# A two-layer adaLN and mixture-of-experts kernel: two-sided decayed sums as a scan of a scan, the shared expert's rows stored as a second summand, routing pieces a step later, VectorE's order written out

## The chip, the cores and the metric

The kernel runs on one core of a Trainium2 chip. The metric is the device time of one execution in microseconds (us). One launch computes everything. The engines are named as in the profile: PE is TensorE's matrix unit (PEld its weight loads), DVE is VectorE, ACT is ScalarE, POOL is GpSimd and SP is SyncE, which here only issues transfers.

## The reference, cut to what matters

There are two layers over x of shape 4 x 512 x 512 (2048 tokens of 512 channels). Each layer first mixes along time, per channel and batch, with a sum that decays in both directions, then runs a mixture of experts and adds the result to x.

```python
def _bi_wkv(r, k, v, w, u, time_emb):          # k and v are the same side input
    tf = sigmoid(sum(time_emb, -1))[:, None, None]
    decay = exp(-exp(w))[None, :] * (0.5 + 0.5 * tf[:, :, 0])
    ek = exp(minimum(k, 30.0)); ekv = ek * v
    # a = a * decay + ekv_t; b = b * decay + ek_t, forward (nf, df) and in reverse (nb, db)
    euk = exp(minimum(u + k, 30.0))
    num = nf + nb - ekv + euk * v
    den = df + db - ek + euk
    return sigmoid(r) * (num / maximum(den, 1e-8)) * (0.8 + 0.2 * tf)

x = x + L0_ffn(L0_cond(x, ...))   # rmsnorm, router to 2 of 8 experts (256 wide), plus a shared expert
x = x + L1_ffn(L1_cond(x, ...))   # router to 6 of 32 experts (352 wide, 512 slots each), plus a shared one
```

## The kernel before, in words

All arithmetic is in float32. The side input is kept turned, channels on partitions, in `kA` (128 x 4 x 2048); the rows of x lie in `acc` (16 tiles of 128 rows). A unit is one batch b and one group c of 128 channels, so a layer has 16 units of 128 x 512.

**Layer 0, the loop over units (L641).** Step n holds pieces of several units. `turn(n + 3)` turns the side input on PE and ACT copies it to `kA`. `front(n + 1)` makes two clamped copies on DVE and `front_exps(n + 1)` takes their exponentials on ACT. `mid(n)` makes two products and four scans on DVE (`scans`, L259): forward and reverse, for the denominator and the numerator, into four tiles. `sums(n - 1)` adds three terms each for `den` and `num` on PE by matmuls with a diagonal matrix (L436 to L438), and ACT then takes a reciprocal in three passes (`r`, L440 to L442). `back(n - 1)` finishes the unit with four operations on DVE (L449 to L452). `num` has one PSUM bank, so the next `num` waits for L451. Between these stand, at fixed steps: `sigmoids` of the next batch; `row_turn` and `row_out` (rows back and stored to `z0d`); `logits0`; the routing of a finished batch in five parts (`route_v`, `route_max`, `route_top`, `route_pos` with `route_pay`, `route_slots`), the last of which writes eight indirect transfers to `table0` from POOL; and the shared expert (`share_up`, `share_silu`, `share_hid`, `share_turn`, `share_down`, `share_add`) for tiles 0 to 5, in pairs that begin at steps 7, 10 and 13. `share_add` adds the shared result to the row of x on DVE and stores the sum to `xa`. A second summand, `xb`, is filled with zeros at the start, by 16 stores on POOL's queue.

**The tail of that stage (L694 to L735).** The last batch is routed; tiles 6 to 12 of the shared expert run; the table is read back; some exponentials of layer 1 (`exps1_upto`) are taken, for which ACT changes its function table and changes it back.

**The routed stage of layer 0 (`routed`, L740).** For each expert, tiles of 128 slots: POOL gathers rows from `z0d` into rows 8 to 15 of `acc` (L768), PE turns them (L781), ACT copies with a scale (L785), PE makes gate and up (L833, L837), POOL multiplies the hidden row (`hrow`, L844), PE turns it (L795) and makes the output (L809), ACT copies it (L811) and POOL adds it by an indirect transfer alternately to `xa` and `xb` (L814). Beside that, DVE runs `wkv1` (L907), the two-sided sums of layer 1, for all 16 units.

**After it.** Three late tiles of the shared expert, then the sum of `xa` and `xb` and layer 1's gating (L962 to L985), the shared expert of layer 1, and its routed stage, which fills the second half of the time.

**What sets the order.** In the first stage the program order of ACT, PE and DVE is kept by hand (`manual_schedule`, L192); POOL and SP are ordered by a planner. In the routed stage of layer 0 POOL, PE and ACT are kept by hand and DVE is ordered by the planner (L936). Each engine runs its queue in order. The transfers of SP share one queue: `load_k` has one buffer `kr`, so the load of the next batch is issued only when all four groups of the present one have been turned.

Of the kernel before, what the change touches and what calls it, by code (L numbers as in the profile page):

```python
# [18 lines left out]
P = 128  # L19
# [6 lines left out]
DEN_MIN = 1e-8  # L26
EXP_LN = "natural_log_exp_and_others"
# [3 lines left out]
def adaln_ffn_kernel(  # L31
# [90 lines left out]
    def load_k(b):  # L122
        kr = wk.tile([P, TB, D], F32, tag="kr", name=f"kr{b}", bufs=1)
        nc.sync.dma_start(kr, kf[b * S : (b + 1) * S, :].rearrange("(i p) c -> p i c", p=P))
        return kr
# [54 lines left out]
    kr = wk.tile([P, TB, D], F32, tag="kr", name="kr0", bufs=1)  # L180
    for i in range(TB):
        nc.scalar.dma_start(kr[:, i, :], kf[i * P : (i + 1) * P, :])
    load_x(0)
    gaten = acc[:E1, NT - 3, :]
# [9 lines left out]
            engines={mybir.EngineType.Activation, mybir.EngineType.PE, mybir.EngineType.DVE}  # L194
# [20 lines left out]
    for l in range(2):  # L215
# [8 lines left out]
        decay.append(dec)  # L224
# [20 lines left out]
    for tb, width in ((table0, 3), (table1, 2)):  # L245
        blank = wk.tile([P, NCOL * width], F32, name=f"blank{width}", tag="lgT", bufs=1)
        bv = blank.rearrange("p (c w) -> p c w", w=width)
        nc.gpsimd.memset(bv, 0.0)
        nc.gpsimd.memset(bv[:, :, 0], EMPTY)
        nc.gpsimd.dma_start(tb.rearrange("(p c) w -> p (c w)", p=P), blank)  # L250
    zero = wk.tile([P, D], F32, name="zero", tag="zr", bufs=TB)
    nc.gpsimd.memset(zero, 0.0)
    for t in range(NT):
        nc.gpsimd.dma_start(xb[t * P : (t + 1) * P, :], zero)


    L = S - 1

    def scans(l, b, c, ek, ekv, df, dx, nf, nx):  # L259

        dec = decay[l][:, c, b : b + 1]
        for v, f, r in ((ek, df, dx), (ekv, nf, nx)):
            nc.vector.tensor_tensor_scan(f, dec.to_broadcast([P, S]), v, 0.0, ALU.mult, ALU.add)
            nc.vector.tensor_tensor_scan(
                r[:, L - 1 :: -1],
                v[:, L:0:-1],
                dec.to_broadcast([P, L]),
                0.0,
                ALU.add,
                ALU.mult,  # L270
            )

# [113 lines left out]
    def turn(n):  # L386

        nonlocal kr
# [4 lines left out]
        for i in range(TB):  # L393
            nc.tensor.transpose(pk[:, i * P : (i + 1) * P], kr[:, i, c * P : (c + 1) * P], ident)
        nc.scalar.copy(kA[:, c, b * S : (b + 1) * S], pk)
        if c == NC - 1 and b + 1 < NB:
            kr = load_k(b + 1)
            load_x(b + 1)

    def front(n):  # L400
# [4 lines left out]
        ek = wk.tile([P, S], F32, tag="ek", name=f"ek{n}", bufs=2)  # L405
        nc.vector.tensor_scalar(ek, kT, 30.0, None, ALU.min)
        euk = wk.tile([P, S], F32, tag="euk", name=f"euk{n}", bufs=3)
        nc.vector.tensor_scalar(euk, kT, uch[0][:, c : c + 1], 30.0, ALU.add, ALU.min)
        fronts[n] = ek, euk

    def front_exps(n):
        if n < NU:
            for v in fronts[n]:
                nc.scalar.activation(v, v, AF.Exp)

    def mid(n):
        b, c = units[n]
        kT = kA[:, c, b * S : (b + 1) * S]
        ek, euk = fronts.pop(n)

        def tmp(tag, bufs=2):
            return wk.tile([P, S], F32, tag=tag, name=f"{tag}{n}", bufs=bufs)

        ekv, eukv = tmp("ekv", 1), tmp("eukv")
        nc.vector.tensor_tensor(ekv, ek, kT, ALU.mult)
        nc.vector.tensor_tensor(eukv, euk, kT, ALU.mult)
        df, dx, nf, nx = tmp("df"), tmp("dx"), tmp("nf"), tmp("nx")
        scans(0, b, c, ek, ekv, df, dx, nf, nx)
        mids[n] = (df, dx, euk), (nf, nx, eukv)

    def sums(n):
# [3 lines left out]
        for p, m, (f, r, o) in zip((den, num), (ident, nfac[:, b, :]), mids.pop(n)):  # L435
            nc.tensor.matmul(p, m, f, start=True, stop=False)  # L436
            nc.tensor.matmul(p[:, :L], m, r[:, :L], start=False, stop=False)
# [36 lines left out]
    def row_out(t, pz):  # L474
        zr = wk.tile([P, D], F32, tag="zr", name=f"zr{t}", bufs=TB)
# [636 lines left out]
```

## Time and profile before

| what | us |
|---|---|
| median of three runs (lowest, highest) | 1581.71 (1581.02, 1586.45) |
| time of the profiled execution | 1576.35 |
| its span, first to last instruction | 1574.6 |
| PE busy in the span | 1441.3 |
| DVE busy | 681.8 |
| ACT busy | 407.1 |
| POOL busy | 582.0 |
| loop over units: last operation of the last `back` begins at | 212.07 |
| PE's first turn of gathered rows (routed stage of layer 0) | 261.40 |
| last multiply of `hrow` in that stage begins at | 519.01 |
| first matmul of layer 1's shared expert | 602.33 |

A line of the timeline has the start, the duration, the engine, the source line, the operation, the tile written and those read, and in brackets the idle time before it and what ended it. In the windows each line has a stretch, its length, the busy time of every engine in it, the clock granted to PE (1.00 is full), the share of time that the transfer engines were busy, and GB/s. In the page's second part each digit is the busy share of one of 40 equal slices of 39.4 us.

### The profile page before, as it was taken

To read this page: it belongs to the slowest core of one execution; us is meant where nothing else is said; L and a number is where in the kernel's file an instruction comes from. 1 tells how busy PE (TensorE), PEld (TensorE's weight loads), DVE (VectorE), ACT (ScalarE), POOL (GpSimd) and SP (SyncE) were. 2 spreads that over 40 slices of the span, in tenths; PEclk is the share of its full clock that TensorE was granted. 3 is DMA by queue.
4 is the path that set the end of the run, shared out by engine and by line. 5 is a ranking of instruction groups with operands and counts; after the bars stand their busy time and mean duration, and the time that the engine had idled before them with its cause. 6 is when DMAs were issued, how large, how long until landed. Compare 5 with 4: busy or idle time off the path is not lost. (4 is left out here: it accounts for less than half of the span.)

```text
span 1574.6 us, 16451 instructions
## 1 busy us (share of the span) xinstructions
PE 1441.3 (92%) x5097; PEld 858.7 (55%) x5097; DVE 681.8 (43%) x1192; ACT 407.1 (26%) x969; POOL 582.0 (37%) x576
## 2 busy tenths in 40 slices
PE   4978988989778698999999999999999999999997
PEld 2444555757556484444444565555655555555554
DVE  6897965999990045341111222222222222222221
ACT  4755634464344232000000111111111111111110
POOL 3010234666555100046662333344334344343332
PEclk8999989999999969999999999999999999999999
DMA  9201114454545652001115464666645495555442
GB/s 350 88 28 41 41 41 167 84 114 69 134 96 133 179 179 92 0 1 56 34 66 163 119 175 100 172 175 163 171 93 156 107 289 107 153 163 145 113 104 36
DMA packets 117179, 184.97 MB, mean 117 GB/s; under 512 B 19928, under 2 KB 65004, under 8 KB 117016
## 3 DMA queue, kind: packets, MB, share of 16 engines
q1 hardware_dynamic: 80120, 122.14, 22.8%
q0 software_dynamic: 36336, 60.04, 20.3%
q8 instruction: 66, 1.08, 0.3%
q10 hardware_dynamic: 576, 1.05, 0.2%
q14 instruction: 81, 0.66, 0.1%
HBM read 152.07 MB, written 52.64 MB: 130 GB/s over the span
## 5 line engine op out<-in xcount | busy, mean ns | idle before, releaser
L809 PE MATMUL pout<-w,hT 128*128 128x512 f32 (+1 forms) x432 | 202.8, 602 | 3.7 <-ACT hT L800 2.9
L833 PE MATMUL pgate<-w,zgT 128*128 128x352 f32 (+1 forms) x656 | 193.2, 438 | 10.9 <-PEq L891 6.7
L837 PE MATMUL pup<-w,zgT 128*128 128x352 f32 (+1 forms) x656 | 189.6, 432 | 0.0
L814 POOL DMA_INDIRECT out_dram<-ob,put x52 | 83.0, 1596 | 281.1 <-DVE ob L813 137.4
L768 POOL DMA_INDIRECT acc<-z1d,put x119 | 123.6, 1038 | 134.7 <-PE pza L781 59.9
L353 POOL DMA_INDIRECT table<-pay,r1sloti x96 | 93.6, 975 | 199.3 <-DVE hid L1061 172.4
L849 DVE SCALAR_TENSOR_TENSOR hrow<-pup,tab,sgt 128x352 f32<-128x352 f32 x84 | 49.1, 584 | 254.1 <-issue 131.2
L833 PEld LDWEIGHTS pgate<-w,zgT 128*128 128x128 f32 x656 | 122.8, 195 | 66.0 <-issue 17.5
L837 PEld LDWEIGHTS pup<-w,zgT 128*128 128x128 f32 x656 | 123.0, 191 | 49.0
L813 DVE COPY ob<-pout 128x512 f32<-128x512 f32 x84 | 58.1, 692 | 174.7 <-PE pout L809 167.3
L809 PEld LDWEIGHTS pout<-w,hT 128*128 128x128 f32 (+1 forms) x432 | 77.5, 194 | 71.3 <-issue 54.7
L353 POOL DMA_INDIRECT table<-r0pay,r0sloti x32 | 36.1, 1128 | 182.8 <-DVE r0sloti L343 137.8
L781 PEld LDWEIGHTS pza<-ident,acc 128*128 128x128 f32 x584 | 72.7, 142 | 53.8 <-issue 27.7
L781 PE MATMUL pza<-ident,acc 128*128 128x128 f32 x584 | 88.2, 276 | 12.9 <-DMA acc<-z0d,put 9.8
L804 ACT COPY hT<-phT 96x128 f32<-96x128 f32 x84 | 22.1, 263 | 287.4 <-DVE hT L802 282.8
L768 POOL DMA_INDIRECT acc<-z0d,put x51 | 69.7, 1367 | 71.9 <-PE pgate L833 27.2
L1058 PE MATMUL g<-zT,w 128*128 128x512 f32 (+1 forms) x192 | 88.6, 605 | 4.4 <-DVE lg L990 4.4
L791 ACT COPY zgT<-pza 128x256 f32<-128x256 f32 x103 | 38.4, 373 | 209.1 <-DVE zgT L790 153.4
L809 PE MATMUL pout<-zT,hT 128*128 128x512 f32 (+1 forms) x192 | 87.8, 592 | 0.0
L795 PE MATMUL phT<-ident,hrow 128*96 128x128 f32 (+1 forms) x322 | 55.9, 276 | 33.3 <-DVEq L891 15.0
L1058 PE MATMUL u<-zT,w 128*128 128x512 f32 (+1 forms) x192 | 86.3, 592 | 0.0
L1067 PE MATMUL o<-w,hid 128*128 128x512 f32 (+1 forms) x192 | 83.8, 592 | 0.0
(277 smaller groups left out, 2158.4 us busy)
## 6 DMA issues: line engine op xcount, KB each, us to landing
w<-in_L_ffn_w_dram SPq DMA_DIRECT2D x44, 704.0 KB
zT<-in_L_ffn_w_dram SPq DMA_DIRECT2D x20, 704.0 KB
w<-in_L_ffn_w_dram SPq DMA_DIRECT2D x22, 512.0 KB
zT<-in_L_ffn_w_dram SPq DMA_DIRECT2D x10, 512.0 KB
w<-in_L_ffn_w_dram SPq DMA_DIRECT2D x22, 192.0 KB
xb<-zero POOLq DMA_DIRECT2D x16, 256.0 KB
acc<-in_x_dram SPq DMA_DIRECT2D x4, 1024.0 KB
z0d<-zr SPq DMA_DIRECT2D x16, 256.0 KB
```

The source lines that it names most:

```text
L353: ins = nc.gpsimd.indirect_dma_start(out=table, out_offset=bass.IndirectOffsetOnAxis(ap=sloti[:, t, j : j + 1], axis=0), in_=pay[:, t, j, ...
L768: nc.gpsimd.indirect_dma_start(out=rows(e, s), out_offset=None, in_=zd, in_offset=bass.IndirectOffsetOnAxis(ap=put_at[:, e * NS + s : e * ...
L781: nc.tensor.transpose(pza[which][:, c * P : (c + 1) * P], rows(e, s)[:, c * P : (c + 1) * P], ident)
L795: nc.tensor.transpose(phT[:m, j * P : (j + 1) * P], hrow[:, f : f + m], ident)
L809: nc.tensor.matmul(po, hT[:m, j, :], dv[:m, j, :], start=(j == 0), stop=(j == nf - 1))
L813: nc.vector.tensor_copy(row, po)
L814: nc.gpsimd.indirect_dma_start(out=outs[n % len(outs)], out_offset=bass.IndirectOffsetOnAxis(ap=at, axis=0), in_=row, in_offset=None, boun ...
L833: nc.tensor.matmul(pg, zt[:, c, :], gv[:, c, :], start=(c == 0), stop=(c == NC - 1))
L837: nc.tensor.matmul(pu, zt[:, c, :], uv[:, c, :], start=(c == 0), stop=(c == NC - 1))
L849: nc.vector.scalar_tensor_tensor(hrow, pu, tab[:, col, 1:2], sgt, ALU.mult, ALU.mult)
L1058: nc.tensor.matmul(p[:m], wv[:, c, f : f + m], zT[:, c, cols], start=(c == 0), stop=(c == NC - 1))
L1067: nc.tensor.matmul(po, hid[:m, j, i * P : (i + 1) * P], dv[:m, j, :], start=(j == 0), stop=(j == len(FCH) - 1))
```

## The change

The reverse scan now runs in place over `ek` and `ekv`, and a forward scan then runs in place over its result. A sum that decays in both directions is such a scan of a scan, up to a factor 1 - decay^2, if the first element of the inner scan is divided by that factor. The factor goes into the exponential as a bias (`lom`, its logarithm); the reciprocal `inv` multiplies column 0 of both rows in one small operation. So each unit has four scans as before, one small operation more, and one tile `v2` for both rows where there were six. PE then adds two terms instead of three. In `wkv1` two additions of 128 x 511 are gone.

The rows of x are stored to `xa` as they are, one batch at a time (steps 2, 6, 10, 14). The shared result goes to `xb`: ACT copies it out of PSUM and SP stores it (`share_put`, in place of `share_add`). Only the three late tiles of `xb` are filled with zeros (step 1), and the tables are blanked at step 2. `kr` has two buffers, and the second batch is loaded at the start. `route_v` moves from the end of step c = 1 to step c = 2, ahead of `front_exps`; `route_top` and `route_pay` from c = 2 to c = 3, ahead of `back`; `route_pos` and `route_slots` from c = 3 to c = 0 of the next batch; the table's transfers are spread over three steps and no longer wait for each other. `share_hid` stands behind `back`. POOL's order is kept by hand too in the first stage, and DVE's in the routed stage of layer 0, with `wkv1(0)` to `wkv1(9)` ahead of it. `zr` has three buffers instead of four.

```diff
-    kr = wk.tile([P, TB, D], F32, tag="kr", name="kr0", bufs=1)
+    krs = [wk.tile([P, TB, D], F32, tag="kr", name="kr0")]
...
     load_x(0)
+    krs.append(load_k(1))
...
-        decay.append(dec)
+        nc.vector.tensor_scalar(dec, dec, NEAR_1, None, ALU.min)
+        om = const.tile([P, NC, B], F32, name=f"om{l}")
+        nc.vector.tensor_scalar(om, dec, -1.0, 1.0, ALU.mult, ALU.add)
+        nc.vector.scalar_tensor_tensor(om, dec, 1.0, om, ALU.add, ALU.mult)
+        lom = const.tile([P, NC, B], F32, name=f"lom{l}")
+        nc.scalar.activation(lom, om, AF.Ln)
+        inv = const.tile([P, NC, B], F32, name=f"inv{l}")
+        nc.vector.reciprocal(inv, om)
+        cap = const.tile([P, NC, B], F32, name=f"cap{l}")
+        nc.vector.tensor_scalar(cap, om, E30, None, ALU.mult)
+        decay.append((dec, cap, lom, inv))
...
-    for t in range(NT):
-        nc.gpsimd.dma_start(xb[t * P : (t + 1) * P, :], zero)
...
-        for v, f, r in ((ek, df, dx), (ekv, nf, nx)):
-            nc.vector.tensor_tensor_scan(f, dec.to_broadcast([P, S]), v, 0.0, ALU.mult, ALU.add)
+        dec, _, _, inv = (m[:, c, b : b + 1] for m in decay[l])
+        for h in range(2):
             nc.vector.tensor_tensor_scan(
-                r[:, L - 1 :: -1],
-                v[:, L:0:-1],
-                dec.to_broadcast([P, L]),
-                0.0,
-                ALU.add,
-                ALU.mult,
+                v[:, h, ::-1], dec.to_broadcast([P, S]), v[:, h, ::-1], 0.0, ALU.mult, ALU.add
             )
+        nc.vector.tensor_scalar(v[:, :, 0], v[:, :, 0], inv, None, ALU.mult)
+        for h in range(2):
+            nc.vector.tensor_tensor_scan(v[:, h, :], dec.to_broadcast([P, S]), v[:, h, :], 0.0, ALU.mult, ALU.add)
...
-            kr = load_k(b + 1)
             load_x(b + 1)
+            if b + 2 < NB:
+                krs.append(load_k(b + 2))
...
-        for p, m, (f, r, o) in zip((den, num), (ident, nfac[:, b, :]), mids.pop(n)):
-            nc.tensor.matmul(p, m, f, start=True, stop=False)
-            nc.tensor.matmul(p[:, :L], m, r[:, :L], start=False, stop=False)
+        for p, m, (d, o) in zip((den, num), (ident, nfac[:, b, :]), mids.pop(n)):
+            nc.tensor.matmul(p, m, d, start=True, stop=False)
             nc.tensor.matmul(p, m, o, start=False, stop=True)
...
-        through(fill_table(table0, sloti, pay, TB, 2, "table0" if b == NB - 1 else None))
+        writes[b] = fill_table(table0, sloti, pay, TB, 2, "table0")
...
-    nc.sync.dma_start(xa[LATE * P :, :], xf[LATE * P :, :])
...
-    def share_add(t):
-        nc.vector.tensor_tensor(acc[:, t, :], shared_up.pop(t), acc[:, t, :], ALU.add)
-        nc.sync.dma_start(xa[t * P : (t + 1) * P, :], acc[:, t, :])
+    def share_put(t):
+
+        so = wk.tile([P, D], F32, tag="so", name=f"so_rows{t}")
+        nc.scalar.copy(so, shared_up.pop(t))
+        nc.sync.dma_start(xb[t * P : (t + 1) * P, :], so)
...
+        if n == 1:
+            for t in range(LATE, NT):
+                nc.gpsimd.dma_start(xb[t * P : (t + 1) * P, :], zero)
+        if n == 2:
+            blank_tables()
+        if c == 2 and b < NB:
+            nc.sync.dma_start(
+                xa[b * S : (b + 1) * S, :].rearrange("(i p) c -> p i c", p=P), acc[:, b * TB : (b + 1) * TB, :]
+            )
         front(n + 1)
+        if c == 2 and b >= 1:
+            route_v(b - 1)
         front_exps(n + 1)
-        if c == 3 and b >= 1:
-            route_pos(b - 1)
+        if c == 0 and b >= 2:
+            route_pos(b - 2)
...
+        for t in pairs0.get(n - 2, ()):
+            share_put(t)
         for t in pairs0.get(n, ()):
             share_silu(t)
...
-        if c == 3 and b >= 1:
-            route_slots(b - 1)
+        if b >= 2 and c < 3:
+            if c == 0:
+                route_slots(b - 2)
+            write_slots(b - 2, 3 if c < 2 else 2)
         if c == 2 and b >= 1:
             route_max(b - 1)
+        if c == 3 and b >= 1:
+            route_top(b - 1)
+            route_pay(b - 1)
...
     for t in (LATE - 2, LATE - 1):
         share_down(t, "den")
-        share_add(t)
+        share_put(t)
     exps1_upto(10)
...
-            nc.vector.tensor_scalar(ek, ek, E30, None, ALU.min)
-            nc.vector.tensor_tensor(ekv, ek, kT, ALU.mult)
-            scans(1, b, c, ek, ekv, df, dx, nf, nx)
-            nc.vector.tensor_tensor(df[:, :L], df[:, :L], dx[:, :L], ALU.add)
-            nc.vector.tensor_tensor(nf[:, :L], nf[:, :L], nx[:, :L], ALU.add)
-            nc.vector.scalar_tensor_tensor(df, euk, E30, df, ALU.min, ALU.add)
+            v = rp.tile([P, 2, S], F32, tag="v2", name=f"v2_{n}", bufs=1)
+            cap = decay[1][1][:, c, b : b + 1]
+            nc.vector.tensor_scalar(v[:, 0, :], ek, cap, None, ALU.min)
+            nc.vector.tensor_tensor(v[:, 1, :], v[:, 0, :], kT, ALU.mult)
+            scans(1, b, c, v)
+            d, s = v[:, 0, :], v[:, 1, :]
+            nc.vector.scalar_tensor_tensor(d, euk, E30, d, ALU.min, ALU.add)
...
-        with tc.manual_schedule(engines={mybir.EngineType.Pool, mybir.EngineType.PE, mybir.EngineType.Activation}):
+        with tc.manual_schedule(
+            engines={
+                mybir.EngineType.Activation, mybir.EngineType.PE, mybir.EngineType.DVE, mybir.EngineType.Pool
+            }
+        ):
+            for n in range(10):
+                wkv1(n)
```

## The prediction

> **What bounds the kernel now.** I first read the busy rows of the page, in slices of 39.4 us.
>
> ```profile
> span 1574.6 us, 16451 instructions
> PE   4978988989778698999999999999999999999997
> DVE  6897965999990045341111222222222222222221
> ```
>
> From the sixteenth slice on PE sets the time and the change touches nothing. What can move lies before 545 us. There DVE is full twice: in the loop over units and, with `wkv1`, from 261 to 471 us. Windows of ten us part the first from its tail:
>
> ```profile
> 30.00:40.00 10.00, 4.24 (x8) 2.26 (x9) 6.47 (x9) 0.59 (x1) 0.00 (x0) 0.50 0.99 374
> 160.00:170.00 10.00, 9.76 (x31) 4.69 (x30) 9.86 (x15) 4.89 (x10) 5.47 (x4) 1.00 0.12 42
> 230.00:240.00 10.00, 10.00 (x39) 7.28 (x38) 3.04 (x10) 1.47 (x4) 6.80 (x7) 0.93 0.09 27
> ```
>
> At 160 us DVE is busy for 9.86 of 10 us: the loop is DVE's. At 230 it is PE that is full and DVE at 3.04: the tail is PE's. At 30 both are idle while transfers run at 374 GB/s. The groups give the unit's pieces (x16: one per unit):
>
> ```profile
> L263 DVE TENSOR_TENSOR_SCAN df<-dec,ek 128x512 f32<-128x512 f32 x16 | 19.5, 1218 | 0.0
> L264 DVE TENSOR_TENSOR_SCAN dx<-ek,dec 128x511 f32<-128x511 f32 x16 | 19.2, 1197 | 0.0
> L612 DVE TENSOR_TENSOR acc<-so,acc 128x512 f32<-128x512 f32 x13 | 8.8, 688 | 6.2 <-PE so L608 5.1 <-issue 0.9
> ```
>
> The change keeps four scans per unit, so DVE's work in the loop hardly falls. What it can take are DVE's waits there, which the timeline of DVE names in brackets:
>
> ```profile
> 43.34 0.69 DVE L449 SCALAR_TENSOR_TENSOR t<-den,r 128x512 f32<-128x512 f32 x1 [6.87 <-ACT r L442]
> 75.78 0.17 DVE L501 TENSOR_SCALAR v<-ssq 128x4 f32<-128x4 f32 x1 [1.77 <-ACT sq L471]
> 123.67 0.17 DVE L501 TENSOR_SCALAR v<-ssq 128x4 f32<-128x4 f32 x1 [1.60 <-ACT sq L471]
> 125.69 0.69 DVE L612 TENSOR_TENSOR acc<-so,acc 128x512 f32<-128x512 f32 x1 [1.02 <-PE so L608]
> 140.78 0.19 DVE L291 TENSOR_REDUCE r0sm<-r0pr 128x4 f32<-128x32 f32 x1 [3.81 <-ACT r0pr L288]
> 187.81 0.19 DVE L516 TENSOR_TENSOR lg<-plt,rs 128x32 f32<-128x32 f32 x1 [1.67 <-PE plt L491]
> 211.35 0.69 DVE L451 TENSOR_TENSOR t<-num,t 128x512 f32<-128x512 f32 x1 [1.44 <-PE num L438]
> ```
>
> The first is a transfer in disguise: PE's turn at 35.76 had waited 8.24 us for `kr`, and `sums` stood behind it.
>
> **The change, part by part.** I follow one moment: PE's start of `share_up(6)`, at 211.15, because from there PE is nearly full. It follows L451 of unit 14's `back` (205.97 to 206.66) and unit 15's `num`.
>
> *Second buffer for `kr`, batch 1 loaded early: -6.9.* Its 1 MB enters SP's queue ahead of the gate, the router and the weights, but 13 zero stores of 256 KB (3.4 MB) and the 0.75 MB copy to `xa` leave the start, so nothing behind it should come later. The moved loads and the four 1 MB stores to `xa` fall where transfers are idle (0.12 at 160 us). If the cover fails, PE waits for the gate a few us, as it did for 1.92 at 15.09.
>
> *Routing a step later: -9.9.* The waits of 1.77, 1.60, 1.02 (that `share_add` is gone), 3.81 and 1.67 are each for something that a step (some 10 us) more makes ready. The operations stay the same in number. `route_slots(2)` now follows unit 14's `back`; before it stood ahead of it: 1.7 us from 202.54 to 204.61, less the 0.4 of another operation between. At this moment that is -1.7; unit 15's `back` gets it instead, and PE has `share_up(6)` to do meanwhile.
>
> *`share_add` off DVE: -2.6.* Six fall in the loop, four before the moment, at 0.64 each (two take 1.28 at 207.30). ACT gets a copy of 0.59 (L811's row) each; it is half idle there (4.89 of 10).
>
> *Two matmul terms instead of three: -1.45.* Unit 15's `num` takes three terms from 206.80 to 211.15, 1.45 each at the low clock there. Elsewhere a term is 0.86, so PE loses 1.7 per unit, which DVE hides and which gives slack.
>
> *The small operation and the order of scans: +4.7.* Independent operations overlap: scans start 1.11 apart with 1.20 of duration. Dependent ones do not: L449, L450 start 0.72 apart, where L425, L426, of equal length, start 0.60 apart. Old scans: 1.14 + 1.115 + 1.11 + 1.115 = 4.48. New: 1.11, then 1.23 until the fix can start, 0.20 for it (small ones take 0.17), then 1.12 and 1.11: 4.77. So 0.29 x 16 = 4.7. The Trainium skill, page "VectorE: DVE Perf Modes", section "The DRAIN you can't avoid", says that the next operation always waits for the pipe to empty; by it the fix would cost its own 0.20, 3.2 in all. The 0.60 against 0.72 here disagrees, so I keep 4.7. No row shows a scan in place. Other in-place rows are as long as the rest (L452 0.691, L451 0.691), so I take no change; the bounds are 0 and +0.3 a scan.
>
> *Preparation of the factors: +1.5.* Ten DVE operations at 0.17 (L221's row) and two logarithms on ACT at 0.21 (L217's), in front of the first `front`, which already waited 0.60. Bounds 0 (fewer transfers bring `kr` sooner; PE waited 2.95 for it) and 2.5.
>
> *What is late next: +3.* Step 13 gives PE `sums` 3.4, turns 2.1, logits 3.4 and `share_up` 6.9, 16 us against DVE's 10. From that, some 3 us of slack and the ACT table change of 1.28, I estimate 2 to 3 us of new wait at step 14. Bounds 0 and 8.
>
> Sum at the moment: -6.9 - 9.9 - 1.7 - 2.6 - 1.45 + 4.7 + 1.5 + 3 = -13.3.
>
> *The tail: 0.* PE keeps the same matmuls. ACT has 0.6 more per tile of 5.4 us. With three `zr` buffers the fourth copy of the last batch may wait 1 us for a store, ahead of `silu`, whose DVE user then waits for routing anyway. POOL's transfers of batch 2 lose their waits (1.43 each); five are left for after the loop, 6.4 us, done before batch 3's slots come.
>
> *Into the routed stage: -2.* These rows decide it (POOL, PE, ACT timelines):
>
> ```profile
> 261.97 1.96 POOL L768 DMA_INDIRECT acc<-z0d,put  x1 [11.37 <-DVE acc L612]
> 270.07 1.11 PE L781 MATMUL pza<-ident,acc 128*128 128x128 f32 x4 [3.70 <-DMA acc<-z0d,put]
> 257.23 1.28 ACT L627 ACT_TABLE_LOAD   x1
> 260.92 1.28 ACT L735 ACT_TABLE_LOAD   x1
> 262.21 1.14 ACT L785 ACTIVATE zgT<-pza,chan 128x128 f32<-128x128 f32 x4
> ```
>
> The second gather waited 11.37 us until a row of `acc` had been added and stored; that reason is gone, and with it PE's waits of 3.70 and 1.07. But ACT must now copy tile 12 (PE done at 260.2) before its exponentials: copy to 260.9, table 1.28, four exponentials 2.4, table 1.28, so the first `zgT` comes at 265.9 instead of 262.21. From tile 12's end to the second tile's gate matmul it was 13.0 us (to 273.16); now I count 6.2 to the first gate matmul, 3.7 for gate and up, 1.0 for the turns: 10.9. A rule speaks against this: the skill's page "ScalarE: Activation LUTs", section "What ACT_TABLE_LOAD costs", gives about 2.66 us per change of set, a drain included. By it the two changes cost 2.8 more and -2 becomes +0.7. Here the row after a load starts 1.29 after it (260.92 to 262.21), so I keep -2.
>
> *`wkv1`: two additions fewer, order fixed: -3.* DVE ends about 20 us sooner, which alone is worth nothing, since tiles wait for PE. But POOL suffers beside it:
>
> ```profile
> 279.00 3.62 POOL L844 TENSOR_TENSOR hrow<-upt,sgt 128x256 f32<-128x256 f32 x1 [2.82 <-ACT upt L843]
> 285.81 0.73 POOL L844 TENSOR_TENSOR hrow<-upt,sgt 128x256 f32<-128x256 f32 x1
> ```
>
> The first fell into DVE's L915 to L919, 3.4 us of elementwise operations without a pause. In the stage `hrow` runs over its 0.73 by 5.8 us in all, and PE waits 11.2 us for it. The train shrinks to about 2.1 us. Bounds: 0, and -8; the tiles may also fall worse, up to +3.
>
> Sum: -13.3 - 2 - 3 = -18.3. The profiled execution takes 1576.35, its span and 1.75 around it, 0.3% under the median of 1581.71. I take the difference for both: 1558 for a profile like it, and 1581.71 - 18.3 = 1563.4 for the median. About 0.5%, or 8 us, is what a measurement here can tell from no change.
>
> **The rivals.**
>
> *PE and ACT take the waits' place, 0.13.* If the wait of 3.81 was PE's load (two silus behind 7 us of matmuls) it comes back elsewhere, and with the upper 8 of new waits and no relief of tiles the sum is -13.3 + 5 - 2 = -10; with +3 in the tiles, -7: about 1575. For it: PE is at 10.00 in some windows. Against it: PE loses 1.7 a unit.
>
> *The tiles gain more, 0.15.* With -8 in them and no new waits in the loop: -13.3 - 3 - 2 - 8 = -26, about 1555. For it: 11.2 us of PE's waits for `hrow`; against it: gathers were also slow (1.96) beside scans, which stay.
>
> *Slower: scans in place take longer, 0.10.* The loop has 64 scans on DVE's own path. From 18.3 / 64 = 0.29 us more per scan, 1.49 in all, nothing is left; at 1.8 us, 64 x 0.6 = 38 more gives +20, 1602. For it: no scan here reads and writes one tile, and its second input is now what the scan before wrote. Against it: the in-place rows above.
>
> That the change does not do what it says needs the second scan to be refused its overlap or the `kr` load to be late; both are inside these cases.
>
> **How the numbers follow.** My own case has 0.62 and gives 1563.4. Faster by over 0.5%: 0.61 of it, 0.15, and a quarter of the first rival: 0.79. Same: 0.11. Slower: 0.10. The range reaches from the second rival with the start's lower bound (1552) to the end of the first (1576); left out are the slower case and the ends.
>
> **What would show it.** Right: no wait near 35 us for `kr`; scans of 1.20; a small operation of 0.17 between two pairs; `share_up(6)` near 198; first gathers right after `put0`, and PE's first turn near 248; L915 and L916 gone and `hrow` nearer 0.73. Wrong: scans over 1.4, waits of DVE in the loop over 8 us in sum, or a PE idle for more than 7 us before the first gate matmul.

## The result and the profile after

The changed kernel takes 1570.34 us (median of 4 runs, 1567.39 to 1572.14), the kernel before beside it 1583.74 (4 runs): ratio 0.991, interval 0.988 to 0.994. In a second, larger series it took 1570.06 (22 runs) against 1577.43 (43 runs): 0.9952, interval 0.9931 to 0.9973. So it is faster, by 7 to 13 us; the forecast of 1563.4 lies 7 below, and 1570 is inside the range. The two profiled executions differ less than the medians, 1572.11 against 1576.35: the one of before was a quick run of its kernel, the one of after a slow one. Runs of one kernel differ by 10 us and more, so what an edit does is read below from moments inside the profile. These scatter too, though less: in a second profile of the changed kernel PE's start of `share_up(6)` is at 201.29 instead of 201.12 and the last `hrow` at 515.06 instead of 515.89, while the loop of before, which the run `before_fixed` below leaves as it is, reaches `share_up(6)` at 213.58 instead of 211.15. So a difference of 2.5 us between two single profiles shows nothing yet.

The page of the changed kernel, first the span and two busy rows:

```profile
span 1570.3 us, 16315 instructions
PE   5788798979788788999999999999999999999997
DVE  7999834999991055431112222222222222222221
```

DVE's row is a little fuller at the left (7999 instead of 6897), because the wait for `kr` is gone. The three windows of before, taken again (columns: length, busy time of PE, PEld, DVE, ACT, POOL, granted clock, DMA share, GB/s):

```profile
30.00:40.00 10.00, 5.69 (x14) 2.40 (x13) 9.76 (x14) 8.88 (x21) 0.00 (x0) 0.91 1.05 403
160.00:170.00 10.00, 10.00 (x43) 6.20 (x42) 9.41 (x15) 6.79 (x15) 5.06 (x5) 0.95 0.30 107
230.00:240.00 10.00, 10.00 (x42) 7.42 (x41) 0.97 (x2) 4.66 (x9) 4.30 (x6) 1.00 0.22 73
```

From 30 to 40 us DVE is now busy for 9.76 of 10 us; at 160 PE is the full engine, not DVE; at 230 the shared additions have left DVE (0.97 instead of 3.04). A unit's scans on DVE's timeline (start, duration, idle time before it in brackets):

```profile
159.09 2.33 DVE L278 TENSOR_TENSOR_SCAN v<-dec,v 128x512 f32<-128x512 f32 x2
161.46 0.23 DVE L281 TENSOR_SCALAR v<-v,inv 128x2 f32<-128x2 f32 x1
161.72 2.34 DVE L283 TENSOR_TENSOR_SCAN v<-dec,v 128x512 f32<-128x512 f32 x2
163.98 0.67 DVE L457 SCALAR_TENSOR_TENSOR t<-den,r 128x512 f32<-128x512 f32 x1
```

Two scans take 2.33 with their overlap, as two of the old ones did (1.11 until the second starts, and its 1.22), so reading and writing one tile costs nothing here; the block takes 163.98 - 159.09 = 4.89 instead of 4.48. Waits of DVE over 0.9 us up to `share_up(6)` are two, both new:

```profile
178.02 0.16 DVE L519 TENSOR_TENSOR v<-v,rsg 128x4 f32<-128x4 f32 x1 [3.88 <-ACT rsg L512]
201.34 0.19 DVE L336 CAST r0posi<-pos 128x32 int32<-128x32 f32 x1 [3.84 <-PE pos L548]
```

Before, six waits of the loop came to 16.7 us (6.87 + 1.77 + 1.60 + 1.02 + 3.81 + 1.67). The border between the tail and the routed stage, on POOL, PE and ACT:

```profile
238.27 1.06 POOL L797 DMA_INDIRECT acc<-z0d,put  x1 [0.82 <-POOL put L747]
252.05 0.66 PE L810 MATMUL pza<-ident,acc 128*128 128x128 f32 x4 [0.72 <-ACT so_rows L628]
257.95 3.75 PE L862 MATMUL pgate<-w,zgT 128*128 128x256 f32 x8 [5.25 <-DMA w<-in_L_ffn_w_up_dram]
251.41 0.59 ACT L628 COPY so_rows<-so 128x512 f32<-128x512 f32 x1 [1.13 <-PE so L622]
252.02 1.28 ACT L643 ACT_TABLE_LOAD   x1
255.88 1.28 ACT L764 ACT_TABLE_LOAD   x1
257.40 1.15 ACT L814 ACTIVATE zgT<-pza,chan 128x128 f32<-128x128 f32 x4 [0.23 <-DMA xb<-so_rows]
```

The gathers go out as soon as their positions are there, and PE's first turn comes at 252.05 instead of 261.40. But the first gate matmul comes only 5.9 us later (before: 1.3), and the second tile's gate at 265.26 instead of 273.16. Of PE's 10.0 us at `share_up(6)` 7.9 are left there, and 3.1 at the last `hrow` (515.89 instead of 519.01). On PE itself less is left at the end of that stage: it turns this last hidden row (`phT`) at 522.66 instead of 523.94, 1.3 earlier, and at 521.85 in the second profile.

What is lost shows in the same stretch of both kernels, from the second gate to the last `hrow`:

```profile
273.16:519.01 245.85, 212.87 (x909) 153.90 (x908) 198.07 (x201) 117.32 (x349) 147.84 (x113) 0.97 0.49 104
265.26:515.89 250.63, 215.86 (x906) 157.17 (x907) 205.73 (x200) 116.86 (x349) 146.73 (x115) 0.94 0.47 102
```

The stretch became 4.8 us longer. PE is busy for 3.0 more with the same matmuls, at a granted clock of 0.94 instead of 0.97; the other 1.8 are idle time. PE's waits from 264 to 522 us (in total, times, longest), three rows of before and then three of after:

```profile
PE phT L795 <- POOL hrow L844: 11.2, 6, 3.8
PE pgate L833 <- PEq L891: 9.2, 3, 3.9
PE pgate L833 <- ACTq L891: 3.9, 4, 1.2
PE pgate L862 <- ACTq L920: 12.5, 4, 4.3
PE pgate L862 <- issue: 5.9, 1, 5.9
PE phT L824 <- POOL hrow L873: 2.8, 3, 1.3
```

PE's wait for `hrow` fell from 11.2 to 2.8, while its waits at the gate matmul, where the expert changes, grew from 13.8 to 22.1 in all. The second of these holds in the second profile too (18.6); the first only in part, for there the wait for `hrow` is 8.4 (11.7 and 13.4 in the other two profiles with the old sums, `before_fixed` and `kr1_early`). The longer pauses account for most of PE's longer busy time: three groups of eight gate matmuls behind such pauses are slow in the changed kernel, one in the kernel before (the last line), by 1.6 to 1.8 us each:

```profile
415.30 3.78 PE L862 MATMUL pgate<-w,zgT 128*128 128x256 f32 x8 [5.87 <-issue]
480.33 3.78 PE L862 MATMUL pgate<-w,zgT 128*128 128x256 f32 x8 [4.28 <-ACTq L920]
509.35 3.60 PE L862 MATMUL pgate<-w,zgT 128*128 128x256 f32 x8 [2.54 <-ACTq L920]
483.91 3.65 PE L833 MATMUL pgate<-w,zgT 128*128 128x256 f32 x8 [3.93 <-PEq L891]
```

Such a group takes 1.97 elsewhere, at a granted clock of 1.00; in these four the clock is 0.50 to 0.52. In seven profiles (these two, `after_again`, `kr1_early`, `before_fixed`, `scan_fixed`, `exps_later`) the groups behind pauses of 3.90 to 5.87 us took 3.35 to 3.78; behind shorter ones some did and some didn't (1.96 behind 2.79 in the kernel before).

Behind the stage the two profiled executions show no gain that belongs to the change. At the first `pt` turn of layer 1 the changed kernel is 0.2 us ahead (552.27 against 552.51), 2.4 in its second profile (550.10). From there to the first matmul of layer 1's shared expert PE does the same 257 matmuls, and their time goes with the granted clock, not with the kernel (before, after, and the changed kernel once more):

```profile
552.51:602.33 49.82, 43.13 (x257) 40.62 (x257) 21.25 (x37) 19.38 (x33) 0.00 (x0) 0.67 0.59 203
552.27:595.97 43.70, 37.49 (x257) 35.03 (x257) 21.12 (x37) 19.25 (x33) 0.00 (x0) 0.77 0.65 227
550.10:599.20 49.10, 43.12 (x257) 40.60 (x257) 21.28 (x37) 19.55 (x33) 0.00 (x0) 0.67 0.58 206
```

This stretch takes 39.05 (clock 0.89) in `kr1_early` and 54.99 (0.56) in `exps_early`. So the 4.2 us between the two profiled executions come from it (6.1 less, of which what follows gives 2.1 back), and that the change is faster rests on the series of runs.

### The profile page after: what moved, and what is told of

It is laid out like the page before. It is cut to its first block, busy times and chain, and to the rows that moved or that the text cites. A ratio compares the mean times of both kernels' runs of the same rounds, so it can differ in the third digit from the quotient of the medians.

```text
span 1570.3 us, 16315 instructions
## 1 busy us (share of the span) xinstructions
PE 1428.1 (91%) x5033; PEld 851.0 (54%) x5033; DVE 678.9 (43%) x1189; ACT 415.7 (26%) x984; POOL 566.4 (36%) x563
## 5 line engine op out<-in xcount | busy, mean ns | idle before, releaser
L862 PE MATMUL pgate<-w,zgT 128*128 128x352 f32 (+1 forms) x656 | 198.6, 448 | 22.6 <-ACTq L920 9.4
L797 POOL DMA_INDIRECT acc<-z0d,put x51 | 62.5, 1226 | 57.9 <-issue 17.3
L819 DVE COPY zgT<-pza 128x256 f32<-128x256 f32 x103 | 42.9, 418 | 88.5 <-PE pup L866 87.8
## 6 DMA issues: line engine op xcount, KB each, us to landing
xa<-acc SPq DMA_DIRECT2D x4, 1024.0 KB, 11.7
```

The lines of the kernel that those rows point to most:

```text
L797: nc.gpsimd.indirect_dma_start(out=rows(e, s), out_offset=None, in_=zd, in_offset=bass.IndirectOffsetOnAxis(ap=put_at[:, e * NS + s : e * ...
L819: nc.vector.tensor_copy(dst[:, :h, :], pza[which][:, : h * P].rearrange("p (c t) -> p c t", c=h))
L862: nc.tensor.matmul(pg, zt[:, c, :], gv[:, c, :], start=(c == 0), stop=(c == NC - 1))
```

## The experiments

All times are us. "The moment" is PE's start of `share_up(6)`: 211.15 before, 201.12 after. The next landmarks are the second gate matmul (273.16, 265.26), the last `hrow` (519.01, 515.89) and the first `pt` turn of layer 1 (552.51, 552.27). Two theories stood against each other at first. A: each edit of the loop gives its own part, as the prediction added them up. B: PE's and DVE's waits there are one resource, so one edit gives what another would have given.

**The second side input early, alone** (`kr1_early`, on the kernel before):

```
+    kr1 = zT[:, :, 3 * S : 4 * S]        # free until batch 3
+    nc.sync.dma_start(kr1, kf[S : 2 * S, :]...)
...
-            kr = load_k(b + 1)
+            kr = kr1 if b == 0 else kr2 if b == 1 else load_k(3)
...
+            if b == 0: kr2 = load_k(2)
```

> The kernel before, with one part of the change alone: batch 1 of the side input is loaded at the start (into a part of zT that is not yet in use), instead of after batch 0 has been turned. Theory A (the wait of 6.87 us at 43 us is that transfer, and the loop carries the time on to the end): share_up(6) at 204 us instead of 211, ratio 0.9955. Rival (the loop takes it back at the next wait, or the start comes later behind one more MB): share_up(6) at 209 or later, ratio 0.999 to 1.000.

Measured: ratio 0.998 (0.996 to 1.001), the moment at 207.94: 3.2 earlier than before, 5.6 earlier than the same loop in `before_fixed`, not 6.9. The wait of 6.87 is gone, and three others stand on DVE's timeline:

```profile
28.91 0.69 DVE L455 SCALAR_TENSOR_TENSOR t<-den,r 128x512 f32<-128x512 f32 x1 [2.80 <-ACT r L448]
71.21 0.17 DVE L507 TENSOR_SCALAR v<-ssq 128x4 f32<-128x4 f32 x1 [2.39 <-ACT sq L477]
120.78 0.17 DVE L507 TENSOR_SCALAR v<-ssq 128x4 f32<-128x4 f32 x1 [3.29 <-ACT sq L477]
```

The second and third were 1.77 and 1.60 before, which looks as if half of the gain were waited away. But `before_fixed`, which has the loop of before without this edit, shows 2.23 and 3.29 at these two places, and 4.55 where before has 6.87. So only the first of the three, 2.80, is new, and this run does not decide between A and B.

**The scan of a scan alone** (`scan_only`, on the kernel before): the new `scans`, factors, bias and two matmul terms in both layers, all else as before.

> The kernel before, with the scan of a scan alone (both layers), the factors in front of it, and two matmul terms instead of three; loads, stores, routing and orders as before. Theory A (DVE sets the loop, so the small operation and the dependent scans cost 0.41 a unit and the factors 2 us, while PE's 1.7 a unit is hidden): share_up(6) at 214 to 218, time 0 to 6 us more than before, ratio 1.000 to 1.004. Rival (PE's relief is what the change lives on): share_up(6) before 209, ratio 0.995 or less.

Measured: ratio 1.035 (1.031 to 1.040), some 56 us slower. The loop is not what is slower: the moment is at 208.49, 2.7 earlier than before, although DVE has more work. The last `hrow` is at 514.16, earlier too. But the first `pt` of layer 1 comes at 620.9 instead of 552.5. None of the theories had this.

**VectorE's order left to the planner** (`planner_dve`, on the changed kernel):

```
-            engines={Activation, PE, DVE, Pool}    # layer 0's tiles, wkv1(0..9) inside
+        for n in range(10): wkv1(n)
+        ... engines={Pool, PE, Activation}
```

> The changed kernel with DVE's order in layer 0's routed stage left to the planner again, as before. Theory A (tiles wait for PE and at expert changes, DVE's order there is worth nothing): within 2 us of the changed kernel from first turn to last hrow. Rival (the fixed order is a part of the gain, or of the loss at expert changes): that stretch differs by 4 us or more from the changed kernel's 264 us.

Measured: ratio 1.041 (1.036 to 1.045), some 65 us slower than the kernel before and 73 slower than the changed one (1643.24 against 1570.06). The waits and two windows of it (columns as above) show how:

```profile
DVE shr L605 <- ACT ssg L599: 158.0, 5, 146.0
400.00:530.00 130.00, 104.36 (x406) 74.67 (x405) 1.17 (x2) 50.17 (x153) 58.16 (x52) 0.88 0.48 115
550.00:600.00 50.00, 0.00 (x0) 0.00 (x0) 49.03 (x53) 0.00 (x0) 0.00 (x0) 0.50 0.00 0
```

The planner put the first late `share_hid` (L605), which can run only at the end of the routed stage, ahead of the units of layer 1 that were still to come. DVE then waits 146 us for it, is busy for 1.17 of 130 us, and does the remaining units after the stage, for 49.03 of 50 us, while every other engine stands still. `scan_only` has the same wait (149.3). With the old scans the planner did the same, but only one operation of layer 1's sums stood behind it, so that the wait cost nothing (kernel before):

```profile
532.70 0.48 DVE L591 SCALAR_TENSOR_TENSOR shr<-pza,rs,ssg 128x256 f32<-128x256 f32 x1 [61.45 <-ACT ssg L585]
533.10 0.74 DVE L922 SCALAR_TENSOR_TENSOR kA<-v,fac,v 128x512 f32<-128x512 f32 x1
```

So Theory A of this run, that the written order is worth nothing, fell: with the new scans it is worth 62 us (`scan_only` against `scan_fixed` below, on two chips) to 73.

**The scan of a scan with VectorE's order written out** (`scan_fixed`): `scan_only`, and the manual order of layer 0's tiles with `wkv1(0..9)` in it, as in the changed kernel. **The order alone** (`before_fixed`): the same, with the scans of before.

> The kernel before, with the scan of a scan in both layers (factors, two matmul terms) as in scan_only, and VectorE's order in layer 0's expert tiles written out as the changed kernel has it; nothing else of the change. Theory A: the loss of scan_only was all VectorE's order that the planner made: here share_up(6) at 208 to 209 as there, last hrow 513 to 518, the first turn of layer 1 (pt) at 547 to 552 instead of 621, ratio 0.995 to 1.000. Theory B: the scan of a scan needs the other edits too: pt over 560, ratio over 1.005.

> The kernel before, with VectorE's order in layer 0's expert tiles written out as the changed kernel has it (units 0 to 9 first, then the experts with the other units at expert 1), the scans as they were. Theory A: the order alone is worth nothing, because the planner's own order for the old scans was near to it: share_up(6) at 211, last hrow 517 to 521, pt 550 to 554, ratio 0.998 to 1.002. Theory B: the written order already gives part of the gain of the tiles: last hrow under 516, ratio under 0.997. Theory C: it costs, because the planner had placed share_hid and the units better: ratio over 1.003.

Measured: `scan_fixed` 0.9954 (0.9935 to 0.9973), the very ratio of the changed kernel in its large series. Moment 206.04, second gate 265.84, last `hrow` 513.73, first `pt` 546.99. `before_fixed` 0.9974 (0.9957 to 0.9990), but no moment of its profile is earlier: 213.58, 274.70, 520.19, 554.80. So the loss of `scan_only` was the planner's order, and the scan of a scan with a fixed order gives by itself all that the whole change gives. How much of that is the scans' stays uncertain: on this chip the medians go from 1578.75 to 1574.14 by the order alone, which no moment explains, and to 1571.79 with the scans; in the profiles it is the scans that bring every moment forward. How they do so is in DVE's busy time (third) from the start to the moment in before, after and `scan_fixed`:

```profile
0.00:211.15 211.15, 167.79 (x554) 90.67 (x555) 176.20 (x367) 117.94 (x215) 36.19 (x55) 0.94 0.29 104
0.00:201.12 201.12, 150.43 (x490) 81.41 (x490) 175.17 (x372) 123.02 (x223) 26.04 (x39) 0.90 0.31 110
0.00:206.04 206.04, 150.04 (x489) 81.88 (x490) 182.15 (x389) 119.03 (x215) 35.38 (x55) 0.90 0.29 107
```

DVE's idle time is 211.15 - 176.20 = 34.95 before, 25.95 after and 23.89 in `scan_fixed`. The scans add 5.95 of work and take 11.1 of waits away (the same two loops in `before_fixed` and `scan_only`: 38.17 and 26.42 idle); routing, its order and the load of `kr` are as before. The waits over 0.9 us that are left:

```profile
41.68 0.69 DVE L451 SCALAR_TENSOR_TENSOR t<-den,r 128x512 f32<-128x512 f32 x1 [2.78 <-ACT r L444]
123.85 0.69 DVE L614 TENSOR_TENSOR acc<-so,acc 128x512 f32<-128x512 f32 x1 [1.02 <-PE so L610]
137.22 0.19 DVE L297 TENSOR_REDUCE r0sm<-r0pr 128x4 f32<-128x32 f32 x1 [1.68 <-ACT r0pr L294]
```

PE has one matmul term less in each of `den` and `num`, 1.7 us per unit, and what DVE waited for came from PE or from ACT behind it. The waits at 75 and 187 us are gone and the one at 140 is shorter without the routing being moved, in both profiles of this loop; the one at 123 is gone here and 1.70 in `scan_only`. This speaks for B. That it is PE's relief is read from these waits: no run takes the terms away alone, and a part of the 11.1 is filled by the 5.95 of new work. The other edits then give 5 us at the moment, all of it work that DVE no longer does or does later (182.15 to 175.17), with 2.1 more waiting. At the second gate these 5 us are gone: 265.84 against 265.26. At the end of the stage PE turns the last hidden row at 518.02 in `scan_fixed` and 518.91 in `scan_only`, but between 520.02 and 522.66 in the five profiles that have the loop and the written order of the changed kernel: there the other edits cost 1 to 5 us.

**Unit 14's last step ahead of the routing of batch 2** (`back_first`, on the changed kernel; it aims at the wait of 3.84):

```
+        if n: back(n - 1)                          # step 15: before, not after
         if c == 3: route_top(b - 1); route_pay(b - 1)
         # step 16: back(15), route_slots(2), share_up(6), then route_pos(2)
```

> The changed kernel with three places moved at the end of the loop: at step 15 back(14) stands ahead of route_top(2) and route_pay(2) on DVE, at step 16 back(15) stands ahead of route_slots(2), and on PE share_up(6) ahead of route_pos(2). Theory A (DVE's wait of 3.84 us for the positions, and num waiting behind five us of routing for back(14), hold PE's tail up): the wait is gone, share_up(6) near 195 instead of 201, first turn of gathered rows near 247 instead of 252, time 4 to 6 us less. Rival (PE's tail then waits for routing of the last batch, which is the same length from another start): share_up(6) earlier but the first turn within 1 us of 252.

Measured: ratio 0.9905 (0.987 to 0.994). The moment is at 193.08, 8.0 earlier, but it is no measure here, since the edit itself puts `share_up(6)` ahead of `route_pos(2)` on PE; PE's first turn of gathered rows is at 247.42, 4.6 earlier. The wait of 3.84 is gone, and the one at step 14 is still there:

```profile
177.43 0.16 DVE L519 TENSOR_TENSOR v<-v,rsg 128x4 f32<-128x4 f32 x1 [3.84 <-ACT rsg L512]
```

Second gate 260.32 (4.9 earlier than after), last `hrow` 510.06 (5.8 earlier). So what is earlier at the border does reach the end of the stage: PE turns the last hidden row at 516.96, 5.7 earlier than after.

**The exponentials ahead of the last shared tiles** (`exps_early`) **and left to expert 1** (`exps_later`), both on the changed kernel, test what holds the first gate:

```
-    exps1_upto(10); preload_act_table_set(...)     # end of the tail
     exps_early: the same two lines ahead of the last two share_down
     exps_later: left out; wkv1(8) and wkv1(9) are done with 10..15 at expert 1
```

> The changed kernel with the last exponentials of the tail (units 8 and 9 of layer 1) and the change of ACT's table put ahead of the last two share_down and share_put, so that they no longer stand between the last copy and the first zgT. Theory A (ACT's queue holds the first gate matmul up, and PE's clock falls in the idle 5.25 us): first gate matmul within 2.5 us of the first turn of gathered rows instead of 5.9, gate and up of the first tile nearer 1.9 each than 3.75 and 2.87, 4 to 6 us less in all. Rival (the gate matmul waits for something else, such as a transfer, or the tiles give it back at the first change of expert): under 1.5 us at the end of the routed stage.

> The changed kernel, with the exponentials of units 8 and 9 (four of 0.71 us and two table changes at the end of the tail) and these units' sums left to expert 1, where the other exponentials of layer 1 are taken. Theory A: ACT's four exponentials and two table changes between the first copied rows and the first gate matmul are what holds the routed stage at its start; without them the first pgate matmul comes within 4.5 us of the first pza turn (5.9 us in the changed kernel), the second tile's gate near 261 instead of 265, and the last hrow near 511 instead of 515: 1566, ratio to the kernel before near 0.990. Theory B: the time is only moved: expert 1 now has sixteen exponentials instead of twelve on ACT, its tiles wait 2.8 us more there, and the last hrow stays at 514 to 516: 1570. The unused table change is then no gain at all.

Measured: `exps_early` 0.9958 (0.9935 to 0.9981), first turn 253.45, first gate 257.42: the copies were held up instead; second gate 263.93, last `hrow` 513.39. `exps_later` 0.9946 (0.9929 to 0.9964), first turn 251.43, first gate 256.62, second gate 262.64, last `hrow` 515.46. The four exponentials and both table changes are out of the way, and the first gate is only 1.3 earlier: 5.2 after the first turn, where Theory A had at most 4.5 and the changed kernel 5.9. The second gate gains 2.6, and the last `hrow` nothing, as Theory B had it. ACT's rows there tell what is behind them:

```profile
250.79 0.58 ACT L628 COPY so_rows<-so 128x512 f32<-128x512 f32 x1 [1.13 <-PE so L622]
256.06 1.14 ACT L812 ACTIVATE zgT<-pza,chan 128x128 f32<-128x128 f32 x4 [4.69 <-DMA xb<-so_rows]
```

ACT does nothing for 4.69 us and waits for a store of `so_rows`. The tile `zgT` has nothing to do with these rows and does not lie where they lay. But `so_rows` is a tile of `wk`, that pool is closed at the end of the tail, and `zgT` is in the pool that is opened after it. In the compiled instruction stream ACT's first write to `zgT` stands behind waits for everything that still used the old pool; in the changed kernel the stores of tiles 11 and 12 are among them, in the kernel before, of SP's stores, only those of `zr`, long done, since its shared rows were stored from `acc`. DVE's first write to the new pool and PE's first gate stand behind the same list, which holds no load of weights, so the releaser named at the gate above is not what it waits for. DVE starts `wkv1` late in the changed kernel:

```profile
257.90 0.49 DVE L942 TENSOR_SCALAR v<-acc,cap 128x512 f32<-128x512 f32 x1 [11.13 <-DMA w<-in_L_ffn_w_up_dram]
```

In `scan_fixed`, which stores from `acc`, ACT and PE go on at once:

```profile
257.19 1.15 ACT L787 ACTIVATE zgT<-pza,chan 128x128 f32<-128x128 f32 x4
257.66 1.97 PE L835 MATMUL pgate<-w,zgT 128*128 128x256 f32 x8 [1.25 <-ACT zgT L787]
265.84 2.77 PE L835 MATMUL pgate<-w,zgT 128*128 128x256 f32 x6
```

After the pause of 5 us PE's first gate takes 3.41 (3.75 in the changed kernel) instead of 1.97, which is another 1.5. The granted clock in the gate (eighth column) is 0.50 in the changed kernel and 1.00 in `scan_fixed`:

```profile
257.95:261.50 3.55, 3.54 (x9) 2.83 (x10) 3.47 (x4) 0.59 (x3) 0.00 (x0) 0.50 0.87 284
257.66:259.50 1.84, 1.84 (x9) 1.63 (x10) 1.84 (x2) 0.68 (x3) 1.34 (x2) 1.00 1.05 378
```

The runs show that the exponentials are not the cause and the trace names the store; `so_rows` in a pool that stays open was not run.

**Both improvements** (`best`: `back_first` with `exps_early`; `best2`: `back_first` with `exps_later`).

> Both of these moves together in the changed kernel. Theory A: 8 to 12 us less than the changed kernel, ratio to before 0.983 to 0.986. Rival: the moves meet in one place, 4 to 6 us less.

> The changed kernel with unit 14's last step ahead of the routing of batch 2 (as in back_first) and units 8 and 9 left to expert 1 (as in exps_later). Theory A: both gains add: share_up(6) at 193, the first pza at 247, second gate near 256, last hrow near 506, 1562, ratio 0.987. Theory B: of back_first's 5 us only those count that the exponentials give back, last hrow near 510, ratio 0.990.

Measured: `best` 0.9917 (0.9895 to 0.9939), last `hrow` 510.03; `best2` 0.9913 (0.9880 to 0.9946), 1565.8, second gate 259.55, last `hrow` 509.74. In both `back_first` gives nearly everything; the exponentials add 0.8 at the second gate in `best2` and nothing at the end. These three are 5 to 6 us ahead of the changed one at the last `hrow`; by the ratio they lead its large series (0.9952), not its first one (0.991); beside `exps_later`'s 1570.66 on the same chip `best2` is 4.9 faster.

**Two more additions per unit of layer 1** (`two_adds`, on the changed kernel: two unused 128x512 sums in every `wkv1`) and **the changed kernel again** (`after_again`):

> The changed kernel with two additions of 128 x 512 per unit put back into layer 1's sums beside the routed stage (their results are not used), so DVE has 22 us more there, in a longer unbroken train of elementwise operations. Theory A (DVE's work there is hidden; trains reach PE only through hrow, and those waits are 3 us now): 0 to 3 us more. Rival (the two additions taken out are a part of the gain, through POOL): 5 us or more, with the sum of hrow over 0.73 each back at 6 us from 4.6.

> The changed kernel as it is, to set the others beside it on one chip. Theory A (the loop over units gave about 10 us, the rest nothing): ratio to before 0.990 to 0.994; share_up(6) on PE again near 201 us, first turn of gathered rows near 252, first matmul of layer 1's shared expert near 596. Theory B (a good part of the gain lies in the routed stage, and the one profiled execution missed it): ratio 0.986 to 0.990, and the stretch from the first turn to the last hrow multiply shorter than the 258 us of before.

Measured: `two_adds` 0.9936 (0.9915 to 0.9957), last `hrow` 513.67; what `hrow` takes over 0.73 comes to 3.1 us in sum, against 4.6 and 5.3 in two profiles of the changed kernel. So DVE's additions there are hidden, and having two fewer gave nothing that can be seen. `after_again`'s numbers stand above.

## Why the prediction was right or wrong, point by point

- **Time and sign: right.** 1570 against 1563.4. At the moment the forecast was -13.3 and the profile has -10.0; the tail and the stage after it were to add -5 and took back 6.9. That the sum came near is in part luck: terms that were too large stood beside others that had the wrong sign or were left at nothing.
- **`kr` -6.9: too large.** Alone it gave 3.2 to 5.6, by which profile of the old loop it is set against. The wait itself was 6.87 in one of these and 4.55 in the other, and a new one of 2.80 came in its place.
- **Routing a step later -9.9: the mechanism is wrong.** The waits did go, but `scan_fixed` loses 11.1 of idle time with the routing unmoved and `kr` as before. As far as the waits show, they were PE's load. The step "PE loses 1.7 per unit, which DVE hides and which gives slack" priced this slack at nothing but 1.45; the gain of the loop hangs on it, if that reading is right. Waits that have one source were counted as if each had its own.
- **New waits +3: 7.7.** The one at step 14 came as described (3.88). The second was not seen: `route_pos(2)` stands behind unit 15's `num` on PE, and `num` waits for unit 14's `back`, which the changed order puts behind 5 us of routing. `back_first` takes it away.
- **Scans +4.7: right in kind.** 4.89 - 4.48 = 0.41 a unit instead of 0.29, 6.6 in all: the small operation takes 0.23, and the second pair starts 0.03 after its end. A dependent operation does wait for the one before, while the pair overlaps (2.33, not 2.40). The Trainium skill, page "VectorE: DVE Perf Modes", section "The DRAIN you can't avoid", says that the next operation waits until the pipe is empty, but adds that one that is not held starts earlier; the prediction left the second half out. In place costs nothing, which ends the rival that was slower.
- **Factors +1.5: not told apart.** The first `front` is at 14.29 instead of 12.04, 2.25 later; but with the old factors it came at 14.60 in `before_fixed` and 11.58 in `kr1_early`.
- **`share_add` -2.6, slots -1.7, terms -1.45:** in DVE's busy time the first two are part of the 7.0 between `scan_fixed` and after; none of the three was run alone.
- **Into the routed stage -2: +0.9.** From tile 12's end (251.33) to the second gate it is now 13.9 (before 13.0; forecast 10.9, and 10.9 in `scan_fixed`). The count of table changes at 1.28 was right: 252.02 to the first `zgT` at 257.40 is 5.4, forecast 5.0. Of the 3.0 over the forecast 0.4 lie ahead of the first gate and 2.6 in the first tile's gate and up, which took 7.3 with the turns instead of 4.7, at the low clock. Missing was also the store ahead of `zgT`, hidden behind the exponentials here but there without them.
- **`wkv1` -3: +4.8 in the stage.** PE's wait for `hrow` did fall, by 8.4 in this pair of profiles and by 2.8 in the second, but it is not the sum of PE's waits: those at the gate grew by 8.3, and slow matmuls follow the long ones. Nor does that wait follow the length of `hrow`: `kr1_early` has 13.4 of it with the old sums, although no `hrow` there takes more than 1.31 (3.1 over 0.73 in sum, against 4.6 in the changed kernel), and `two_adds` shows that the number of additions isn't what counts. The granted clock of the stage is 0.93 to 0.95 in every kernel with the new scans and 0.97, 0.96 and 0.95 in the three with the old ones, whose stretch took 245.5 to 249.3. Why the waits at the gate grew is open.
- **"Order fixed" was priced at nothing**, as one half of a clause. It is what keeps the change from being some 60 us slower. The chance of slower, 0.10, was put on the scans in place, and the real danger was the planner's place for one instruction.
- **What the loop's moments don't explain:** from the last `hrow` to the first `pt` after took 36.4 (35.0 in the second profile), before 33.5. Of the 2.9 between, 1.8 are that POOL had run further ahead of PE (`phT` comes 6.8 instead of 4.9 behind this `hrow`), and the first 32 matmuls of the late tiles took 8.19 instead of 7.07 (7.07 in the second profile). Up to the first `pt` the two profiles of the changed kernel are 0.2 and 2.4 ahead; where the rest of the 7 to 13 us between the medians lies is open.

## What to carry to other kernels

Waits of one engine for the same other engine may be one sum: before they are added up, ask which edit relieves the engine that is waited for, and count only that. When one stage's operations change in length, look at where a planner puts an instruction that can't run for a long time; one such instruction at the head of a queue can cost more than all that was tuned. Rows that are moved from a long-lived tile to one of a pool that closes bring their store into the path of the first instruction after it. And a second profile of code that was not changed tells how far a moment or a wait moves by itself: here 2.5 us, as much as several of the effects that were looked for.

## What was not expected of the hardware

- The 3.62 us that one `hrow` took beside five elementwise operations of the old `wkv1` did not come back: in the two other profiles with the old `wkv1` the longest is 1.31 (`kr1_early`) and 1.72 (`before_fixed`), in the two of the changed kernel 1.62 and 1.68. So it was not the rule for these operations.
- The two table changes with nothing between them and the next operation cost 1.28 each: `zgT` follows the load by 1.29 in `scan_fixed` (255.90 to 257.19), which is less than half of the 2.66 that the Trainium skill, "ScalarE: Activation LUTs", section "What ACT_TABLE_LOAD costs", gives with its drain.
- In `exps_later` ACT's wait for the last store ended 4.7 us after its rows were copied, where these stores take 2.0 in the median from issue to landing. This one was issued 0.66 behind 512 KB of the next expert's weights on the same queue and ahead of two more such loads; its own landing is not in the trace, so how much of the 4.7 is these loads stays open.
